# Layer 1's experts by blocks of one expert's tokens, in a four-layer transformer kernel on one core

## The chip, the cores and the metric

The kernel runs on 1 core of one Trainium2 chip. Its time is the device time of one execution in microseconds (us). Before the change it is 931.48 us, the median of 3 runs (926.2 to 931.48).

The engines are named as the profile names them: PE is TensorE (matrix products; PEld is its loading of weights), DVE is VectorE, ACT is ScalarE, POOL is GpSimd and SP is SyncE, which here only issues DMAs. Each engine works through a queue of its own in order.

## The reference, cut to what matters

The input x holds 16 sequences of 128 tokens with 128 features, in 32-bit floats. There are four layers. Each adds to x a gated attention of the normed x with a context, and then a gated feed-forward part of the normed x. `_layernorm` works on each token by itself.

```python
x = x + jnp.tanh(g_xattn[0]) * _L0_xattn_ref(_layernorm(x), ctx)           # linear attention
x = x + jnp.tanh(g_ffn[0])   * _L0_ffn_ref(_layernorm(x), ...)             # 8 experts, 2 of them per token
x = x + jnp.tanh(g_xattn[1]) * _L1_xattn_ref(_layernorm(x), ctx, ...)      # one head
x = x + jnp.tanh(g_ffn[1])   * _L1_ffn_ref(_layernorm(x), ...)             # 16 experts, 4 per token, 2 shared
x = x + jnp.tanh(g_xattn[2]) * _L2_xattn_ref(_layernorm(x), ctx, ctx, ...) # 16 heads, mask
x = x + jnp.tanh(g_ffn[2])   * _L2_ffn_ref(_layernorm(x), ...)             # 64 slots
x = x + jnp.tanh(g_xattn[3]) * _L3_xattn_ref(_layernorm(x), ctx, ctx, ...) # 16 heads, two scales
x = x + jnp.tanh(g_ffn[3])   * _L3_ffn_ref(_layernorm(x), ...)             # 32 experts, 8 per token, 1 shared
```

The part that the change is about is the feed-forward part of layer 1. An expert has a hidden width of 128.

```python
topk_idx, tw = _route(x, router_w, bias)   # sigmoid scores, the best 2 of 4 groups, then 4 of 16 experts
combine = (jax.nn.one_hot(topk_idx, 16) * tw[..., None]).sum(1)   # zero for 12 of 16 experts
h = jnp.einsum('td,edf->etf', x, gate_w)
u = jnp.einsum('td,edf->etf', x, up_w)
y = jnp.einsum('etf,efd->etd', jax.nn.silu(h) * u, down_w)
routed = jnp.einsum('etd,te->td', y, combine)
sh = jax.nn.silu(x @ sh_gate_w) * (x @ sh_up_w) @ sh_down_w
return routed + sh
```

Every token is multiplied with every expert here, and the products of 12 of the 16 experts get the weight zero.

## The kernel before, in words

The 16 sequences are four groups (0 to 3) of four sequences; a group is 512 tokens. `X[g]` holds a group's x in the core's memory all the time, as 128 partitions by 4 sequences by 128 features. A feed-forward part is computed for one group at a time, an attention likewise.

**Dense steps.** `experts` (L1028) walks over `ORDER`: layer 0 for group 0 only, layer 1 for groups 0 to 3, layer 3 for groups 0 to 3. For each of them it takes steps `n` over 128 hidden units each: 16 in layer 0, 18 in layer 1 (the 2 shared ones first), 17 in layer 3. `gated` (L440) issues a step's gate product (L445) and up product (L446), each with 512 columns; ACT applies the activation (L450, or L453 for silu), DVE forms `sg` (L451) and `h` (L457), and POOL or DVE multiplies `h` by the tokens' routing weights (`hw`, L461). `down` (L1033) adds the step's down product (L1036) to an accumulator, `LAG` = 2 steps later. At the end of a group `end` (L1042) transposes the sum (L1046) and adds it to X (L272). The PE instructions of this stream are held in order by `in_turn`.

**Routing.** `routing` (L839) norms a group (`normed`, L249: DVE, a power on POOL at L260, DVE at L264), transposes it (L244), computes the router's logits and weights (`weights_1`, L561, with `grouped_route`), and `spread` (L411) writes the weights to memory and loads each expert's row back, broadcast over all partitions (L428, 16 loads of 256 KB for layer 1).

**Blocks in layer 0.** Groups 1 to 3 of layer 0 (12 batches of 128 tokens) are computed otherwise. `choose_0` (L855) norms and transposes the three groups, computes all weights, counts on PE how many tokens chose each expert (L872 to L875), and gives each pair of token and expert a row in a table of 31 blocks of 128 rows, each block of one expert. POOL then scatters the tokens to these rows in the chip's memory by 24 indirect DMAs (L901), and each engine that needs it loads the blocks' weight positions into registers (L919). `blocks_0` (L930) loads four blocks of rows at a time (L959), transposes them (L966), copies the block's expert weights to a fixed place (L982), multiplies (L988), applies the activation (L995, L996), multiplies by the down weights (L943) and writes the rows to a second table (L951). `return_0` (L1008) fetches for each token its two rows by indirect DMAs on POOL (L1017, 24 of them) and adds them to X with their weights on DVE (L1024).

**What sets the order.** The attentions are issued by the main program (the loops at the end of the function), and `until` lets the stream of experts go on just far enough for the next attention. Inside `experts`, `steps` names the dense step after which a piece of another work is issued: pieces of `choose_0`, of `routing`, of `return_0` and of `slots_2` (layer 2's feed-forward part). A scheduler then orders each engine's queue: an instruction issued earlier in the program goes first among those that it reckons ready. `side` picks the PSUM banks: "m" for attention (four banks), "x" for experts (three banks), plus one bank for accumulators. Attention 2 of a group follows layer 1 of that group, attention 3 follows its slots, and layer 3 follows attention 3.

Of the kernel before, what the change touches and what calls it, by code (L numbers as in the profile page):

```python
# [36 lines left out]
NBLK = (2 * NT * P + 8 * (P - 1)) // P  # L37
# [22 lines left out]
def flamingo(ctx, tc, x_in, ctx_in, mask_in, w1, w2, w3, wslot, wsmall, slots, cols_in, rows_in, consts_in,  # L60
# [152 lines left out]
    xd, yd = [dram.tile([NBLK * P, D], F32, tag=n, name=n, bufs=1) for n in ("xd", "yd")]  # L213
    zeros, z0 = vp[:].rearrange("p t x -> p (t x)"), xd[:].rearrange("(p r) d -> p (r d)", p=P)
    for i in range(0, NBLK * D, GB * VB):
        n = min(GB * VB, NBLK * D - i)
        nc.scalar.dma_start(z0[:, i:i + n], zeros[:, :n])
# [12 lines left out]
    counted = const.tile([P, NBLK], I32, tag="counted", name="counted")  # L230
    nc.gpsimd.iota(counted[:], pattern=[[1, NBLK]], base=0, channel_multiplier=0)
    count = const.tile([P, NBLK], F32, tag="count", name="count")
# [5 lines left out]


# [9 lines left out]
    def normed(g, xn=None):  # L249
# [10 lines left out]
        nc.gpsimd.tensor_tensor(rs[:], ve[:], neghalf[:], ALU.pow)  # L260
# [13 lines left out]
    def add_row(g, r):  # L274
        nc.gpsimd.tensor_tensor(X[g][:], X[g][:], bc(r[:], 1, GB), ALU.add)
# [79 lines left out]
    def logits_of(xnT, w, n):  # L355
        p = split(mm_tile()[:, :GB * n])
        for t in range(GB):
            mm(p[:, t, :], xnT[:, t * P:(t + 1) * P], w)
        return p
# [23 lines left out]
    def grouped_route(p, bias, n, ngrp, top_grp, lt, fill, topk, tag, times):  # L383

        sc = small.tile([P, GB, n], F32, tag="sc", name="sc")
        nc.scalar.activation(sc[:], p, AF.Tanh, scale=0.5)
        nc.vector.tensor_scalar(sc[:], sc[:], 0.5, 0.5, ALU.mult, ALU.add)
        s = small.tile([P, GB, n], F32, tag="s", name="s", bufs=1)
        nc.vector.tensor_tensor(s[:], sc[:], bc(bias, 1, GB), ALU.add)

        s3 = s[:].rearrange("p t (g k) -> p (t g) k", g=ngrp)
        pairs = small.tile([P, GB * ngrp, 6], F32, tag="pairs", name="pairs", bufs=1)
# [3 lines left out]
        more, gs = room(GB, ngrp, top_grp if ngrp == 8 else 8, tag="gs", name="gs")  # L396
        nc.vector.tensor_reduce(gs, pairs[:].rearrange("p (t g) k -> p t g k", t=GB), AX.X, ALU.max)
        gm = first(more, ngrp, top_grp)[0] if ngrp == 8 else earlier_or_greater(gs, ngrp, lt, top_grp, "g" + tag)

        gf = small.tile([P, GB, ngrp], F32, tag="gf", name="gf")  # L400
        nc.vector.tensor_scalar(gf[:], gm[:], fill, fill, ALU.mult, ALU.subtract)
        more, m = room(GB, n, topk, tag="m", name="m", bufs=1)
# [4 lines left out]
        tw = small.tile([P, GB, n], F32, tag="tw", name="tw", bufs=1)  # L407
        nc.vector.tensor_tensor(tw[:], sc[:], sel[:], ALU.mult)
        return over_sum(tw, n, "comb", act, eps=1e-20, times=times)
# [29 lines left out]

    def gated(chain, w, xnT, cb, tanh, banks, vector):  # L440
# [409 lines left out]

    places = {}

    def choose_0():  # L855

# [171 lines left out]
    def experts():  # L1028
# [88 lines left out]
        while behind:  # L1117
            down()
# [216 lines left out]
```

## Time and profile before

| | |
|---|---|
| median of 3 runs | 931.48 us (926.2 to 931.48) |
| the profiled execution's own time | 930.84 us |
| its span in the profile | 929.1 us |
| mean granted PE clock | 0.965 |
| busy: PE, DVE, ACT, POOL | 90%, 62%, 28%, 30% |
| instructions | 16015 |
| moved by DMA | 62.12 MB, mean 67 GB/s |
| chain that ended last: PE, DVE, POOL, issue, ACT, DMA | 54%, 21%, 8%, 8%, 4%, 2% |

The ends of the groups can be read from the transposes at L1046. They start at 109.3 us (layer 0, group 0); 279.2, 370.8, 480.4 and 607.3 (layer 1, groups 0 to 3); 729.3, 816.9, 883.7 and 924.4 (layer 3, groups 0 to 3). The blocks of layer 0 run from 110 to 170 us.

How to read it: a group of instructions is given by line, engine, operation, the tiles written and read, the count, the busy time and the mean duration, and then the idle time of the engine before them with what ended it. "issue" means that nothing in the profile explains a wait. A 128x128 by 128x512 product in 32-bit floats appears as two PE records. In answers in order of time the first two numbers are the start and the length in us, and a bracket at the end is the idle time before.

### The profile page before, as it was taken

What the parts mean: (1) busy time and instruction counts of PE and PEld (TensorE: products, weight loads), DVE (VectorE), ACT (ScalarE), POOL (GpSimd) and SP (SyncE); (2) the same over time, 40 slices, a digit from 0 to 9 for tenths busy, and PEclk for the clock granted to TensorE, in tenths of its full rate; (3) what the DMA queues carried; (4) which work ended last, traced back from release to release, by engine and by line L of the source; (5) the groups of instructions that cost most, each with busy time, mean ns of one, the idle gap of its engine ahead of it and who ended that gap; (6) DMA issues with size and microseconds to landing.
All of it is one profiled execution on the core that took longest, in us unless ns stands there. A gap on an engine that the chain in (4) does not pass through costs nothing.

```text
span 929.1 us, 16015 instructions
## 1 busy us (share of the span) xinstructions
PE 834.3 (90%) x6183; PEld 468.5 (50%) x6183; DVE 580.6 (62%) x1628; ACT 259.3 (28%) x457; POOL 282.6 (30%) x283
## 2 busy tenths in 40 slices
PE   3889399877999999999899999999989998999997
PEld 3554289534544554455455555555554554554443
DVE  4756252566977475666675866677666668566622
ACT  1222166221321222232223222223222232322321
POOL 3326521353233124311421113421114223313443
PEclk9979699978999999999999999999999999999999
DMA  9711212552121012100202112310002111211231
GB/s 305 211 17 40 64 46 79 159 162 63 24 69 44 27 35 80 46 21 28 69 35 67 35 47 62 123 37 24 24 24 72 35 48 46 76 51 49 94 103 34
DMA packets 55677, 62.12 MB, mean 67 GB/s; under 512 B 14312, under 2 KB 33512, under 8 KB 55472
## 3 DMA queue, kind: packets, MB, share of 16 engines
q1 hardware_dynamic: 53776, 55.90, 19.9%
q0 software_dynamic: 1536, 3.15, 1.1%
q10 hardware_dynamic: 288, 2.03, 0.6%
q8 instruction: 49, 0.80, 0.4%
q14 instruction: 28, 0.23, 0.1%
HBM read 53.97 MB, written 7.09 MB: 66 GB/s over the span
## 4 chain that ended last, share of the span: by engine, by line
PE 54%; DVE 21%; POOL 8%; issue 8%; ACT 4%; DMA 2%; another core or an unknown queue 1%; SPq 1%; POOLq 0%; DVEq 0%; ACTq 0%
PE mm L108 8%; PE acc L1036 7%; PE pg L445 7%; PE pu L446 7%; POOL hw L461 3%; DVE sg L451 3%; PE mm L593 2%; PE po L487 2%; DVE h L457 2%; DVE mp L481 2%; POOL rs L260 2%; POOL y L1017 2%; DVE xn L264 2%; PE tr L244 2%; PE po L490 2%
## 5 line engine op out<-in xcount | busy, mean ns | idle before, releaser
L461 POOL TENSOR_TENSOR hw<-h,cb 128x512 f32<-128x512 f32 x126 | 161.0, 1278 | 459.4 <-DVE h L457 348.1
L446 PE MATMUL pu<-xnTx,wall 128*128 128x512 f32 x288 | 156.4, 626 | 14.9 <-DVE sg L451 13.1
L1036 PE MATMUL acc<-hw,wall 128*128 128x512 f32 x288 | 153.9, 618 | 10.6 <-DVE h L457 9.9
L445 PE MATMUL pg<-xnTx,wall 128*128 128x512 f32 x288 | 154.8, 620 | 7.8 <-issue 4.7
L450 ACT ACTIVATE sg<-pg 128x512 f32<-128x512 f32 x123 | 73.6, 598 | 244.7 <-PE pg L445 230.5
L457 DVE TENSOR_TENSOR h<-sg,pu 128x512 f32<-128x512 f32 x145 | 99.1, 683 | 60.9 <-PE pu L446 40.7
L451 DVE SCALAR_TENSOR_TENSOR sg<-sg,pg 128x512 f32<-128x512 f32 x123 | 83.6, 680 | 51.4 <-ACT sg L450 51.3
L1036 PEld LDWEIGHTS acc<-hw,wall 128*128 128x128 f32 x288 | 55.1, 198 | 71.3 <-issue 53.0
L446 PEld LDWEIGHTS pu<-xnTx,wall 128*128 128x128 f32 x288 | 52.4, 197 | 75.9 <-issue 39.1
L481 DVE TENSOR_REDUCE mp<-mm 128x4 f32<-128x512 f32 (+1 forms) x112 | 65.8, 645 | 21.1 <-PE mm L593 19.9
L445 PEld LDWEIGHTS pg<-xnTx,wall 128*128 128x128 f32 x288 | 50.1, 194 | 50.2 <-issue 35.1
L495 DVE RECIPROCAL rcw<-po 128x128 f32<-128x128 f32 (+1 forms) x28 | 25.2, 900 | 57.1 <-PE po L490 44.8
L264 DVE TENSOR_SCALAR xn<-x,mv,rs 128x128 f32<-128x128 f32 x116 | 40.3, 399 | 25.4 <-POOL rs L260 25.4
L615 ACT ACTIVATE pts<-mm 128x512 f32<-128x512 f32 x64 | 33.6, 602 | 73.3 <-PE mm L609 73.3
L487 PE MATMUL po<-pts,vp 128*32 128x128 f32 (+1 forms) x896 | 46.1, 274 | 7.6 <-ACT pts L615 6.7
L260 POOL TENSOR_TENSOR rs<-ve,neghalf 128x4 f32<-128x4 f32 x32 | 33.2, 1037 | 61.8 <-DVE ve L258 61.7
L490 PE MATMUL po<-pts,own 128*32 128x128 f32 (+1 forms) x896 | 44.3, 266 | 0.5 <-issue 0.5
L453 ACT ACTIVATE sg<-pg 128x512 f32<-128x512 f32 x33 | 19.7, 597 | 67.9 <-PE pg L445 58.4
L487 PEld LDWEIGHTS po<-pts,vp 128*32 128x32 f32 (+1 forms) x896 | 21.3, 108 | 29.9 <-ACT pts L615 14.0
L254 DVE BATCH_NORM_STATS2 st<-x 128x6 f32<-128x128 f32 x128 | 29.5, 280 | 10.2 <-DMA x<-in_x 9.9
L593 PE MATMUL mm<-kTm,qT 32*128 32x256 f32 x256 | 30.5, 413 | 0.0
L1017 POOL DMA_INDIRECT y<-yd,to x24 | 23.7, 987 | 21.7 <-DMA yd<-yb 8.8
(335 smaller groups left out, 1226.0 us busy)
## 6 DMA issues: line engine op xcount, KB each, us to landing
cb<-combD SPq DMA_DIRECT2D x72, 256.0 KB
cb<-combD SPq DMA_DIRECT2D x128, 128.0 KB
wall<-in_gu SPq DMA_DIRECT2D x24, 256.0 KB
wall<-in_dn SPq DMA_DIRECT2D x12, 256.0 KB
xb<-xd SPq DMA_DIRECT2D x7, 256.0 KB
yd<-yb SPq DMA_DIRECT2D x7, 256.0 KB
xd<-vp ACTq DMA_DIRECT2D x1, 1072.0 KB
x<-in_x SPq DMA_DIRECT2D x4, 256.0 KB
```

The source lines that it names most:

```text
L108: nc.tensor.matmul(out=o, lhsT=l, rhs=r, start=start, stop=stop)
L264: nc.vector.tensor_scalar(xn[:, t, :], x[:, t, :], mv[:, t, 0:1], rs[:, t:t + 1], ALU.subtract, ALU.mult)
L445: in_turn(chain, nc.tensor.matmul(out=pg[:], lhsT=w[:, 0], rhs=xnT[:], start=True, stop=True))
L446: in_turn(chain, nc.tensor.matmul(out=pu[:], lhsT=w[:, 1], rhs=xnT[:], start=True, stop=True))
L450: nc.scalar.activation(sg[:], pg[:], AF.Tanh, scale=0.5)
L451: nc.vector.scalar_tensor_tensor(sg[:], sg[:], 1.0, pg[:], ALU.add, ALU.mult)
L457: nc.vector.tensor_tensor(h[:], sg[:], pu[:], ALU.mult)
L461: (nc.vector if vector else nc.gpsimd).tensor_tensor(hw[:], h[:], cb[:], ALU.mult)
L481: nc.vector.tensor_reduce(mp[:, 0:n, 32 * i + 16:32 * i + 18], src, AX.X, ALU.max)
L487: in_turn(chain, nc.tensor.matmul(out=po[32 * jj:32 * jj + 32, 0, :], lhsT=vcols, rhs=pts, start=first, stop=last, skip_group_check=True))
L490: in_turn(chain, nc.tensor.matmul(out=po[32 * jj:32 * jj + 32, 1, :], lhsT=own[rows, r, :], rhs=pts, start=False, stop=last, skip_group_ch ...
L1036: in_turn(chain, nc.tensor.matmul(out=acc[0][:], lhsT=w[:, 2], rhs=h[:], start=n == 0, stop=last))
```

## The change

The new kernel treats groups 1 to 3 of layer 1 as layer 0 was treated. `choose_0`, `blocks_0` and `return_0` become `choose`, `blocks` and `fetch` for both layers.

- In layer 1 a token has four chosen experts, so the 12 batches need 48 scatters and 48 fetches, and the table has 63 blocks. A block of layer 1 has one gate, one up and one down product of 128 by 128 by 128; four blocks share a pass. Its weights are copied by POOL alone, two blocks to a tile. The activation is tanh on ACT and a product on DVE, as in layer 1's dense steps.
- Group 0 of layer 1 stays dense, with all `hw` products on DVE. Groups 1 to 3 run only the two shared steps densely (`stream(..., some=2)` with no routing weights): groups 1 and 2 right after group 0, group 3 after the blocks.
- The rows' table of layer 1 is filled with zeros by DMAs on SP in the program's opening part.
- `choose(1)` is issued after steps 10, 13, 15, 16, 17 and 17 of group 0; its first 12 scatters come with the last of these, the other 36 after the shared steps.
- `fetch` asks for four sets of four rows ahead, and adds one set at a time after named steps. By `behind_of`, an indirect DMA follows the latest power or row addition on POOL, an addition follows the latest `h` on DVE, and the first transposes of layer 1's blocks follow the last products of attention 2 of group 0.
- The later order is new: attention 2 of group 0, then the blocks with the slots of group 0 beside them, attention 3 of group 0, attention 2 of groups 1 and 2, attention 3 of group 1, attention 2 of group 3, attention 3 of groups 2 and 3. The slots of group g+1 go with layer 3 of group g. Layer 3's weights take the place of layer 1's after the blocks.
- The block positions are loaded into registers at the start of the blocks, at most 32 at a time.

```diff
-NBLK = (2 * NT * P + 8 * (P - 1)) // P
+EXPERTS, CHOSEN = {0: 8, 1: 16}, {0: 2, 1: 4}
+NBLK = {i: (CHOSEN[i] * NT * P + EXPERTS[i] * (P - 1)) // P for i in (0, 1)}
...
-        nc.gpsimd.tensor_tensor(rs[:], ve[:], neghalf[:], ALU.pow)
+        latest["row"] = nc.gpsimd.tensor_tensor(rs[:], ve[:], neghalf[:], ALU.pow).ins
...
+    def behind_of(what, ins):
+
+        if what in latest:
+            tc.add_manual_dep(ins.ins, latest[what].name,
+                              mybir.DependencyInfo(mybir.DependencyClass.NoSync, mybir.DependencyReason.DATA),
+                              reason="behind")
...
         for t in range(NT):
-            for k in range(2):
-                apart("xd", nc.gpsimd.indirect_dma_start(
-                    out=xd[:], out_offset=bass.IndirectOffsetOnAxis(ap=to[:, k, t:t + 1], axis=0), in_=xs[:, t, :],
-                    in_offset=None))
+            for i in range(k):
+                ins = nc.gpsimd.indirect_dma_start(
+                    out=xd[layer][:], out_offset=bass.IndirectOffsetOnAxis(ap=to[:, i, t:t + 1], axis=0),
+                    in_=xs[t // GB][:, t % GB, :], in_offset=None)
+                behind_of("row", ins)
+                apart(f"xd{layer}", ins)
+            if layer == 1 and t == 2:
+                yield
...
+        m, nc_ = (2, 2) if layer == 0 else (4, 1)
...
+                    ins = nc.tensor.transpose(pt[:, i * P:(i + 1) * P], xb[:, i, :], ident[:])
+                    if not chain and layer:
+                        behind_of("a2", ins)
+                    in_turn(chain, ins)
...
+                    half = wb[:, i % 2 * 2 * P:(i % 2 + 1) * 2 * P]
+                    src = wall[:, bass.ds(whose[b0 + i], 2 * CH)].rearrange("p (a f) -> p a f", a=2)
+                    copy(half.rearrange("p (a f) -> p a f", a=2), src[:, :, 0:P])
...
+    def fetch(layer):
+        to, by, _ = places[layer]
+        n = CHOSEN[layer]
+        held = []
+
+        def add():
+            g, y, k = held.pop(0)
+            for t in range(GB):
+                i = (g - BYE) * GB + t
+                ins = nc.vector.scalar_tensor_tensor(X[g][:, t, :], y[:, t, :], by[:, k, i:i + 1], X[g][:, t, :], ALU.mult,
+                                                     ALU.add)
+                behind_of("h", ins)
+            return g if k == n - 1 else None
...
+        todo = [(g, k) for g in range(BYE, NG) for k in range(n)]
+        for _ in range(4):
+            ask_next()
+        yield
+        while held:
+            yield add()
+
+            if len(held) in (2, 0) and todo:
+                ask_next()
+                ask_next()
...
+        at(steps, "x", fetch(0), RETURN_0, lambda g: g and (0, g))
+        at(steps, "m", ch, CHOOSE_1)
+        yield from stream(1, 0, *routed.pop((1, 0)), steps, moving=range(18))
+        for g in EARLY:
+            yield from stream(1, g, turned[g], None, {}, 2)
+        yield from flush()
+        side[0] = "m"
+        for _ in ch:
+            pass
+        sl = slots_2(0)
+        for n, _ in enumerate(blocks(1)):
+            side[0] = "s"
+            if n in SLOTS_0:
+                next(sl)
+                yield from shown(("slots", 0) if n == SLOTS_0[-1] else None)
+            side[0] = "m"
+        back, nxt = fetch(1), routing(3, 0)
+        side[0] = "x"
+        for step in (nxt, nxt, back):
+            next(step)
+        for g in range(BYE, NG):
+            if g not in EARLY:
+                yield from stream(1, g, turned[g], None, {}, 2)
+        if len(EARLY) < NG - BYE:
+            yield from flush()
+        for i in range(4):
+            side[0] = "x"
+            g = next(back)
+            yield from shown(g and (1, g))
+            side[0] = "x"
+            if i in (0, 1):
+                next(nxt)
+        loaded(3)
...
+    RETURN_0, CHOOSE_1 = (0, 3, 5, 6, 7, 9, 10), (10, 13, 15, 16, 17, 17)
+    EARLY = (1, 2)
+    SLOTS_0 = range(10)
+    RETURN_1 = (5, 6, 6, 7, 7, 8, 8, 9)
+    SLOTS = {1: (10, 11, 12, 12, 13, 13, 14, 15, 15, 16), 2: range(1, 11), 3: range(10)}
+    ROUTE_3 = (16, 16, 16, 16)
+    ATTEND = {0: ((2, 11), (3, 16))}
...
-    for g in range(NG + 1):
-        if g < NG:
+    for stage, g in ((2, 0), (3, 0), (2, 1), (2, 2), (3, 1), (2, 3), (3, 2), (3, 3)):
+        if stage == 2:
             until(1, g)
             attention_2(g)
-        if g > 0:
-            until("slots", g - 1)
-            attention_3(g - 1)
+        else:
+            until("slots", g)
+            attention_3(g)
```

## The prediction

> **What bounds the kernel now.** I read the page's busy table, then the costliest groups, then stages cut at the ends of the expert layers' token groups, then single engines in order of time where a stage showed a hole. TensorE (PE) is busy 90% of the span, and the dense expert matmuls lead the groups; an indirect DMA costs GpSimd (POOL) about 1 us.
>
> ```profile
> span 929.1 us, 16015 instructions
> PE 834.3 (90%) x6183; PEld 468.5 (50%) x6183; DVE 580.6 (62%) x1628; ACT 259.3 (28%) x457; POOL 282.6 (30%) x283
> ...
> L446 PE MATMUL pu<-xnTx,wall 128*128 128x512 f32 x288 | 156.4, 626 | 14.9 <-DVE sg L451 13.1
> L1017 POOL DMA_INDIRECT y<-yd,to x24 | 23.7, 987 | 21.7 <-DMA yd<-yb 8.8
> ```
>
> The stages follow (columns: stage, length, busy us of PE, PEld, DVE, ACT, POOL, granted clock, DMA share, GB/s). From 279.2 on PE is the bound in each. Only the stage in which layer 0's rows come back (170.4 to 215) has holes and a lower clock.
>
> ```profile
> 170.40:215.00 44.60, 31.88 (x76) 13.66 (x74) 23.03 (x64) 10.64 (x17) 26.02 (x27) 0.85 0.59 169
> 279.20:370.80 91.60, 86.60 (x645) 43.00 (x644) 59.51 (x137) 21.35 (x39) 25.53 (x23) 1.00 0.15 47
> 370.80:480.40 109.60, 103.56 (x749) 55.56 (x748) 74.32 (x184) 29.47 (x51) 28.64 (x27) 1.00 0.13 40
> 883.70:929.00 45.30, 40.14 (x99) 17.71 (x97) 11.75 (x17) 8.94 (x15) 18.97 (x15) 0.99 0.22 70
> ```
>
> The price of a dense step, from PE in order of time near the end, where nothing else runs: each of three matmuls is two records, and starts lie 0.86 us apart, so a step (gate, up, down) is 2.575 us.
>
> ```profile
> 894.43 1.02 PE L1036 MATMUL acc<-hw,wall 128*128 128x512 f32 x2
> 895.29 1.02 PE L445 MATMUL pg<-xnTx,wall 128*128 128x512 f32 x2
> 896.15 1.02 PE L446 MATMUL pu<-xnTx,wall 128*128 128x512 f32 x2
> 897.00 1.02 PE L1036 MATMUL acc<-hw,wall 128*128 128x512 f32 x2
> ```
>
> The price of blocks, from layer 0's: four blocks between two groups of transposes take 5.85 us (144.59 to 150.44). Eight records, four 128-column matmuls, take 0.89; four transposes 0.44.
>
> ```profile
> 144.59 0.60 PE L966 MATMUL tr<-ident,xb 128*128 128x128 f32 x4
> 145.03 1.06 PE L943 MATMUL acc<-wall,h 128*128 x8
> ...
> 150.44 0.60 PE L966 MATMUL tr<-ident,xb 128*128 128x128 f32 x4
> ```
>
> PE's waits while rows are fetched, and the pace of scatters on POOL (0.96 and a pause of 0.30: 1.263 us each):
>
> ```profile
> 184.33 2.08 PE L446 MATMUL pu<-xnTx,wall 128*128 128x512 f32 x2 [4.34 <-DVE sg L451]
> 192.69 2.07 PE L445 MATMUL pg<-xnTx,wall 128*128 128x512 f32 x2 [4.74 <-issue]
> 217.66 2.08 PE L446 MATMUL pu<-xnTx,wall 128*128 128x512 f32 x2 [5.17 <-DVE sg L451]
> ```
> ```profile
> 102.66 0.96 POOL L901 DMA_INDIRECT xd<-xs,to  x1 [0.30 <-issue]
> 103.93 0.95 POOL L901 DMA_INDIRECT xd<-xs,to  x1 [0.30 <-issue]
> ```
>
> **The change part by part.** The sum is made in the profiled execution (span 929.1, its own time 930.84, so 1.7 beside the span); the median of the runs is 931.48, 0.6 above it.
>
> *Work taken from PE.* Layer 1 ran 18 dense steps for each of four groups. Groups 1 to 3 keep 2 shared steps each; 48 steps go: 48 x 2.575 = 123.6 us. In come at most 63 blocks. Four of them are 12 matmuls and four transposes, 3 x 0.89 + 0.44 = 3.12 us, so 63/4 x 3.12 = 49.2 us. Three routings leave (transposes 0.43, logits 0.80, spread 0.44: 1.7 each); the choice for twelve batches brings 12 transposes, logits and a count that took 2.9 us in layer 0 (66.70 to 69.60; 3.5 taken for twice the columns), together 7.2. PE is 72 us lighter. The other engines also lose: 48 times 1.36 us on VectorE (DVE), 0.60 on ScalarE (ACT), 1.28 mostly on POOL.
>
> *Until the fourth group leaves attention 1.* The last block of layer 0 ends at 170.4 and I move nothing before it. Its block names are now loaded at the blocks' start (one load took 2.6 to 3.0 us on each queue); PE stood still 9.9 us there in the profile, which covers it. If that cover goes, it costs 3. The zeros for layer 1's rows (4 MB, four DMAs on SP) go out beside a DMA share of 0.25 or less; cost 0, at most 10. Fetches now stand behind the latest GpSimd row operation and additions behind the latest h, so the three PE waits shown (4.34 + 4.74 + 5.17 = 14.2 us) should mostly go. Attention 1 of group 3 ended at 271; I take 257, with bounds of 250 (the clock of 0.85 recovers too) and 271 (no gain: all hw products of group 0 move to DVE, six more of 0.69, where DVE was busy 51.7 of 64.2).
>
> *The new scatter.* After 257 everything goes through one chain: norm 4.6 (281.7 to 286.3), transposes and copy 1.7, logits and tanh 1.2, choice 10 (6.9 for four batches, 161.98 to 168.85; twelve have three times the columns, so 6.9 to 13), counts 3.5, places 4.8 (69.78 to 74.62): 25.8. Then 48 scatters at 1.263 = 60.6, then landing, load and first transpose 5.3 (104.88 to 110.19). First block at 257 + 91.7 = 349, bounds 339 and 363. Attention 2 of group 0 lies beside it (281.7 to 338.9 in the profile, with dense steps in its gaps), the four early shared steps too, but there is no further dense work. Roughly 30 us of PE idle is the price of this place. In POOL's queue attention 2's power and row operations stand before the 36 later scatters, by the added dependency; the first 12 can hold them 15 us, which is inside the bounds.
>
> *From the first block on.* From 279.2 to the end was 649.9 us. Attention 2 of group 0 with 18 steps is over by then: minus its stage, 91.6. Of the other 36 steps two shared ones stay: minus 34 x 2.575 = 87.6. Blocks: plus 49.2. Two routings: minus 3.4. Idle that went with the removed work (stages from 370.8: busy 522.9 of 558.3, 6.4%): minus 2.7. Rest: 514.
>
> *Fetching back.* A last copy out lands after 5.1 us (170.9 to 176.0), 16 gathers of 1.25 give 20, the last landing and additions 3: 28 us from the last block to attention 2 of group 1. Cover: two shared steps (5.2), routing 1.7, the rest of attention 3 of group 0, and layer 3's first steps if its weights (3.1 MB, behind the last block now, at some 176 GB/s) have come. Bounds 5 and 28; I take 16. The other 32 gathers lie beside attention 2 of group 1. The 48 additions (0.34 each, 16 us) go to DVE, which loses more than that; they cost something only if one waits for its rows at the head of DVE's queue, in the bound.
>
> *Order of later stages.* Attention 3 of group 1 now runs with layer 3's group 0 spent and group 1 not routed; attention 3 of group 0 took 38 us with about six dense steps in it (470 to 509). Plus 8, between 0 and 12. SP's queue loses 51 DMAs of the three spreads (48 of 256 KB) and gains 32 block loads and stores; nothing new stands in front of a weight load but these. The copies of block weights (63 on POOL, half of a 0.61 us copy) lie under PE; the final group is unchanged.
>
> *Clock.* After a hole the same matmul pair took 2.08 instead of 1.02 us for about two pairs: plus 2, between 0 and 6.
>
> Sum: 349 + 514 + 16 + 8 + 2 = 889, plus 1.7 beside the span: 891 us. All low ends give 339 + 514 + 5 + 1.7 = 860, all high ends 363 + 514 + 28 + 12 + 6 + 1.7 = 925.
>
> **A rule that speaks against the change.** The trace shows scatters at 0.96 us (24 of them, 1.23 at most) though DVE was busy 8.4 of 16 us beside them (76 to 92). The Trainium skill's page "SBUF — State Buffer", section "SBUF: two separate sides", says that descriptors of a DMA issued from GpSimd cannot be written while VectorE holds the shared port in a two-port mode. The page gives 3100 against 620 ns; 64 DMAs on the path with 2.5 us more each would make the sum about 1050, an estimate from that page that no row here supports.
>
> **Rivals.**
> 1. *The scatter's hole is filled*: slots and attention 3 of group 0 need only attention 2 and could run before the blocks, so some 30 us return, partly lost again in the fetch (10), while the remaining fetch wait hides: 891 - 30 = 861. For: both are emitted early in the block stage. Against: the blocks' first transposes are emitted before them, and PE takes its queue in order.
> 2. *Slower*: indirect DMAs beside busy attention take longer. The place is POOL, 48 scatters and the first 16 gathers on the path. From 0.63 us more each (1.9 instead of 1.263) the gain is gone; doubled, 64 x 1.26 = 81, 972 us. For: a gather took 1.51 once, and tiny VectorE operations (128x4, 0.17) took 1.14 beside POOL work. Against: the medians, 0.958 and 0.952.
> 3. *PE's queue waits twice in full*: attention 2 of group 1 stands before layer 3's steps while its rows come, and the choice gains nothing: 349 to 363 (+14), fetch at 28 (+12), attention 3 at 12 (+4): 921. For: PE waited for h or sg three times in the first return. Against: shared steps are put between.
> 4. *Blocks save less than they should*: PE matmul time isn't the block's limit, four blocks take layer 0's 5.85 us, for three PSUM banks serve gate, up and transposes. Plus 15.75 x 2.73 = 43: 934. For: only the three banks. Against: per four blocks DVE has 1.4, ACT 1.8, POOL 1.3 us, and layer 0's 61 us stage was 98% busy.
>
> **How the numbers follow.** Forecast 0.48 (its own range 870 to 910), rival 1 0.17, rival 2 0.10, rival 3 0.17, rival 4 0.08. About 1% is what a measurement of this kernel can tell from no change: below 922 is faster, above 941 slower. Faster: forecast, rival 1 and most of rival 3 (0.13): 0.78. Same: the rest of rival 3 and most of rival 4: 0.10. Slower: rival 2 and the tail of rival 4: 0.12. The range 852 to 930 takes in both ends of the sum and rivals 1 and 3; it leaves out rival 2, rival 4 and a little below, 0.18 to 0.2.
>
> **What would show it.** PE matmul records fall by 48 x 6 and rise by 63 x 7 or so; four blocks take about 3.1 us; 48 scatters run at 1.26 us in one row of POOL with PE idle some 30 us before the first block near 349; a hole of 10 to 20 us on PE before attention 2 of group 1; no PE wait over 4 us in layer 0's return. It would be wrong if scatters stretch, if the hole before the blocks is filled, or if PE stands before layer 3's first group for longer than 28 us.

## The result, and the profile after

The changed kernel takes 1056.24 us (median of 4 runs, 1051.29 to 1059.9) against 931.48 (median of 4, 926.2 to 931.88): ratio 1.1351, 95% interval 1.1289 to 1.1413. The prediction was 891, with a range of 852 to 930. It was wrong by 165 us and on the wrong side.

The page of the changed kernel first (columns as before). PE is less busy, as the change wanted, but by 22 us (834.3 before) and not by the 72 of the prediction, and in a longer span, at a mean granted clock of 0.874 (0.965 before). The 48 new scatters (and 24 old ones) keep their 0.97 us. New is the last entry of the L510 line: PE idle ahead of attention 2's weighted products, ended by "issue", by nothing that the profile shows.

```profile
span 1054.4 us, 16557 instructions
...
PE 812.1 (77%) x6350; PEld 500.7 (47%) x6350; DVE 570.0 (54%) x1630; ACT 256.6 (24%) x451; POOL 316.5 (30%) x371
...
L938 POOL DMA_INDIRECT xd<-xs,to x72 | 70.0, 973 | 30.0 <-issue 21.3
...
L510 PE MATMUL po<-pts,own 128*32 128x128 f32 (+1 forms) x896 | 52.8, 288 | 24.2 <-issue 24.2
```

Then the stages of the changed kernel (stage, length, busy us of PE, PEld, DVE, ACT, POOL, clock, DMA share, GB/s), cut at the end of layer 1's group 0, at the first block, at the end of the shared steps of group 3, at the first exponentials of attention 2 of group 1, at the end of layer 3's group 0 and at its last.

```profile
272.50:397.30 124.80, 61.04 (x566) 35.19 (x565) 42.62 (x142) 11.15 (x20) 53.90 (x65) 0.70 0.09 32
397.30:501.60 104.30, 93.69 (x1024) 79.77 (x1022) 61.06 (x144) 41.44 (x73) 26.39 (x59) 0.97 0.30 89
501.60:557.00 55.40, 19.31 (x82) 9.78 (x85) 24.53 (x89) 3.07 (x6) 31.48 (x34) 0.66 0.30 98
557.00:784.20 227.20, 192.27 (x2074) 110.24 (x2067) 141.68 (x350) 50.03 (x93) 37.20 (x35) 0.89 0.08 26
784.20:1049.70 265.50, 220.68 (x1574) 118.76 (x1572) 137.31 (x362) 64.25 (x113) 70.24 (x57) 0.89 0.14 45
```

Three stretches stand out. From 272 to 397 PE does 61 us of work in 125: the transposes of the first block start at 397.3 and not at 349. From 502 to 557, while rows are fetched, it does 19 in 55. The last stretch, from layer 3's group 0 to its last group, takes 265.5 us; before the change it took 195.1 (729.3 to 924.4), and the change does not touch its dense steps.

What stands still in the first stretch is seen on PE in order of time (start, length, the idle time ahead in the bracket). The products of attention 2 first come eight at a time, then one by one, and the time between two starts grows from 0.7 to 3.5 us. Nothing that the profile shows explains these waits: the bracket names no engine. GpSimd's row of scatters lies beside it, from 291.3 to 352.

```profile
310.71 0.65 PE L507 MATMUL po<-pts,vp 128*32 128x128 f32 x8
311.14 0.64 PE L510 MATMUL po<-pts,own 128*32 128x128 f32 x4
312.67 0.37 PE L510 MATMUL po<-pts,own 128*32 128x128 f32 x1 [0.89 <-issue]
...
320.45 0.37 PE L507 MATMUL po<-pts,vp 128*32 128x128 f32 x1 [1.03 <-issue]
...
331.68 0.37 PE L507 MATMUL po<-pts,vp 128*32 128x128 f32 x1 [2.43 <-issue]
...
355.48 0.37 PE L510 MATMUL po<-pts,own 128*32 128x128 f32 x1 [3.12 <-issue]
```

**The theories.** *Hold-up*: beside a long row of indirect DMAs the other engines get their instructions late, so that attention 2 of group 0 hides nothing of the row. *Order* (the rival): the loss lies in the later order, where attention, slots and routing of a group now stand one after the other, and the dense steps that were taken away had been their cover. Both turned out true: the first is worth 53 us, and only on some chips, the second 66 to 86 us, by the way it is counted.

### The profile page after: what moved, and what is told of

Same layout as the page of the kernel before. It is cut to its first block, busy times and chain, and to the rows that moved or that the text cites. A ratio compares the mean times of both kernels' runs of the same rounds, so it can differ in the third digit from the quotient of the medians.

```text
span 1054.4 us, 16557 instructions
## 1 busy us (share of the span) xinstructions
PE 812.1 (77%) x6350; PEld 500.7 (47%) x6350; DVE 570.0 (54%) x1630; ACT 256.6 (24%) x451; POOL 316.5 (30%) x371
## 4 chain that ended last, share of the span: by engine, by line
PE 24%; DVE 11%; issue 9%; POOL 6%; ACT 1%; DMA 1%; another core or an unknown queue 1%; POOLq 0%; DVEq 0%; ACTq 0%
PE mm L109 4%; PE pg L464 3%; POOL y L1117 3%; PE pu L465 3%; PE acc L1144 3%; DVE mp L501 2%; PE po L507 2%; POOL hw L481 1%; PE po L510 1%; PE mm L612 1%; DVE h L476 1%; POOL rs L268 1%; PE tr L109 1%; PE mm L774 1%; DVE rep L362 1%
## 5 line engine op out<-in xcount | busy, mean ns | idle before, releaser
L481 POOL TENSOR_TENSOR hw<-h,cb 128x512 f32<-128x512 f32 x61 | 77.8, 1276 | 277.5 <-DVE h L476 258.4
L465 PE MATMUL pu<-xnTx,wall 128*128 128x512 f32 x192 | 105.0, 630 | 14.4 <-DVE sg L470 7.7
L1144 PE MATMUL acc<-hw,wall 128*128 128x512 f32 x192 | 103.5, 624 | 6.5 <-DVE hw L481 4.8
L464 PE MATMUL pg<-xnTx,wall 128*128 128x512 f32 x192 | 104.9, 629 | 3.3 <-DVE h L476 3.3
L476 DVE TENSOR_TENSOR h<-sg,pu 128x512 f32<-128x512 f32 x97 | 66.3, 684 | 62.2 <-PE pu L465 47.8
L1117 POOL DMA_INDIRECT y<-yd,to x72 | 70.7, 982 | 80.5 <-DVE x L1097 45.6
L469 ACT ACTIVATE sg<-pg 128x512 f32<-128x512 f32 x75 | 44.8, 597 | 203.9 <-PE pg L464 182.0
L938 POOL DMA_INDIRECT xd<-xs,to x72 | 70.0, 973 | 30.0 <-issue 21.3
L470 DVE SCALAR_TENSOR_TENSOR sg<-sg,pg 128x512 f32<-128x512 f32 x75 | 51.0, 682 | 41.0 <-ACT sg L469 40.9
L510 PE MATMUL po<-pts,own 128*32 128x128 f32 (+1 forms) x896 | 52.8, 288 | 24.2 <-issue 24.2
L510 PEld LDWEIGHTS po<-pts,own 128*32 128x32 f32 (+1 forms) x896 | 30.9, 119 | 26.4 <-issue 25.9
```

Of the source, the lines that this page charges most:

```text
L464: in_turn(chain, nc.tensor.matmul(out=pg[:], lhsT=w[:, 0], rhs=xnT[:], start=True, stop=True))
L465: in_turn(chain, nc.tensor.matmul(out=pu[:], lhsT=w[:, 1], rhs=xnT[:], start=True, stop=True))
L470: nc.vector.scalar_tensor_tensor(sg[:], sg[:], 1.0, pg[:], ALU.add, ALU.mult)
L476: ins = nc.vector.tensor_tensor(h[:], sg[:], pu[:], ALU.mult)
L481: (nc.vector if vector else nc.gpsimd).tensor_tensor(hw[:], h[:], cb[:], ALU.mult)
L510: in_turn(chain, nc.tensor.matmul(out=po[32 * jj:32 * jj + 32, 1, :], lhsT=own[rows, r, :], rhs=pts, start=False, stop=last, skip_group_ch ...
```

## The experiments

Each group of kernels below ran on one chip, with a run of the kernel before that took 927 to 933 us on every one of them. The chips are lettered in the order of their use. Except for the kernel of layer 0's new return (chip B), each kernel ran once in its group; one of them, the changed kernel without scatters, ran on two chips and took 990.43 and 992.09 us. "The record" means the runs of the first section, whose chip was not noted.

### Chip A: the change's parts, and the row of scatters by itself

*The kernel before without the 48 dense steps.*

```diff
+                if not (layer == 1 and g >= BYE and n >= 2):
                     banks = [bank("pg", wide), bank("pu", wide)]
...
+                                                stop=n == 1 if cut else last))
```

> The kernel before, in which groups 1 to 3 of layer 1 compute only their two shared steps (48 dense steps are left out, everything else keeps its place). This prices what the change took from TensorE without anything that it added. By the prediction's own terms: 48 x 2.575 = 123.6 us come off the path, so 808 us. By the rival theory that dense steps were the cover of attention chains, and TensorE merely waits where they stood: only about half comes off, 860 to 880 us.

845.25 us: 86.3 came off, not 123.6. The rival was half right about the cover (its 860 to 880 was too high). In the stretch from layer 1's group 0 to layer 3's group 0, PE's idle time rose from 25.9 us (450.1 minus 424.2) to 46.3 (364.7 minus 318.4). Its busy time there fell by 105.8 us and not by 123.6: the matmuls that stayed took longer (the 512 products of L609 302 ns each for 283), at a granted clock of 0.94 where it was 1.00.

*The changed kernel without layer 1's scatters, and without scatters, blocks and fetches.*

```diff
-            for i in range(k):
+            for i in range(k if layer == 0 else 0):
...
-        for n, _ in enumerate(blocks(1)):
+        for n, _ in enumerate([None] * 16):
```

> The changed kernel without layer 1's 48 scatters (its blocks read the zeros of the table, so layer 1's routed part of groups 1 to 3 is missing from the output); all else is unchanged. Theory 1 (the row of scatters holds up attention 2 of group 0 beside it): attention 2 of group 0 runs its 57 us from 297 on, and the blocks start some 58 us earlier: 1056 - 58 = 998 us. Theory 2 (attention 2 waits for something else): the blocks start where they did, since they stand behind attention 2 of group 0: 1045 to 1056 us.

990.43 us, 66 less than on record; this seemed to fit the hold-up, but the 1056 comes from another chip (see chip F).

> The changed kernel without layer 1's scatters, blocks, fetches and additions (the routed part of groups 1 to 3 is missing from the output); the choice, the shared steps, the slots and the later order stay. It prices the later order beside the kernel before without its 48 dense steps, which does the same work. If the order costs little, the two lie within 20 us (the return of layer 0 is better here). If the order is the larger part of the loss (attention and routing one after the other with no dense steps in their gaps), this one is 50 us or more above it, about 880 to 900 us.

931.42 us, 86 us above the kernel before without its 48 steps, which does nearly the same work (three routings of layer 1 where this one has the choice): the order is expensive, more than expected. Its last stretch takes 263.4 us (661.4 to 924.8); in the kernel before without its steps it takes 193.1. So 70 of the 86 us lie there, with no block, scatter or fetch of layer 1 in the kernel at all: 36 us more busy time of PE (219.1 for 183.0; the slots of one more group now stand in this stretch) and 34 us more idle time. Blocks and fetches together cost 990.43 - 931.42 = 59.

*A row of indirect DMAs by itself.*

> A kernel of its own that computes nothing of the reference: ten phases one after the other, each with the same chain of 24 turns (eight small matmuls on TensorE, one tanh on ScalarE, one addition on VectorE). Beside it GpSimd's queue holds, phase by phase: nothing; 48 scatters; 48 gathers; 48 copies; 24 scatters with a copy after each; 48 scatters of 64-byte rows; 48 direct writes from GpSimd's queue; 48 direct writes from SP's queue; 12 scatters; nothing. Theory 1 (a long unbroken row of indirect DMAs holds up the instructions of the other engines, whatever they wait for): the phases with 48 scatters and 48 gathers take clearly longer than the first, as a turn that takes 2 to 3 us runs at a fraction of its pace from about the 15th DMA on, and recovers after the 48th (60 us of DMAs, so a phase of 55 us grows to about 100); the phases with copies, with SP's writes and with 12 scatters keep the first phase's length within 5 us. Theory 2 (the engines waited in the changed kernel for something in GpSimd's own queue, or for data): all phases keep the first one's length within 5 us, or reach the series' 60 us and no more.

All phases took 122.8 to 124.8 us (the last, which also writes the output, left out), with the 48 scatters 122.8 and with the copies 124.8. No hold-up: theory 2 seemed right, but the later chips show that this was one on which no row held anything up.

### Chip B: halves, and a denser chain

> The first of these kernels of its own showed no effect of a row of 48 indirect DMAs on a chain that issues 18 instructions in 5 us. This one computes nothing of the reference either: seven phases with the same chain of 12 turns, each of 64 tiny matmuls, four tanh and four additions, so that every engine issues many more instructions in a microsecond; beside it GpSimd's queue holds nothing, 48 scatters, 48 gathers, 48 copies, 24 scatters with a copy after each; then SP's queue 48 direct writes; then nothing. Theory 1a (while indirect DMAs run in a row, new instructions reach the engines at a limited pace, some 0.7 us each, once those at hand are used up): the phases with 48 scatters and 48 gathers are longer than the first by 30 us or more, those with copies and SP's writes are not. Theory 1b (the hold-up has to do with where the real kernel's tables and instructions lie, or with what its queue holds, and not with the DMAs as such): all seven phases have one length within 5 us.

The phases took 339.4 us alone, **382.0 beside 48 scatters, 383.4 beside 48 gathers**, 339.5 beside 48 copies, 339.8 beside 24 scatters with a copy of 512 elements after each (1.77 us each), 339.6 beside SP's 48 writes. This is theory 1a, and the same picture as in the kernel. PE in order of time, in the phase with scatters (row from 344.0 to 404.4):

```profile
354.83 9.11 PE L114 MATMUL ps<-a,ident 128*128 128x8 f32 x42
364.60 0.17 PE L114 MATMUL ps<-a,ident 128*128 128x8 f32 x1 [0.66 <-issue]
...
371.66 0.38 PE L114 MATMUL ps<-a,ident 128*128 128x8 f32 x1 [1.24 <-issue]
...
391.29 0.17 PE L114 MATMUL ps<-a,ident 128*128 128x8 f32 x1 [2.63 <-issue]
...
411.59 2.08 PE L114 MATMUL ps<-a,ident 128*128 128x8 f32 x9 [0.32 <-issue]
```

For 20 us matmuls follow each other at 0.21 us; then one comes each 0.7, 1.4, 2.1 and 2.8 us, steps of 0.70; 7 us after the row's last DMA all is as before.

*Half the scatters, and no fetches.*

```diff
-            for i in range(k):
+            for i in range(2):
```

> The changed kernel with 24 of layer 1's 48 scatters (two of a token's four rows; half of the routed part of groups 1 to 3 is missing from the output). Without any scatter it was 990 us, with all 1056. If attention 2 of group 0 is held up for as long as the row lasts beyond its first dozen DMAs, half the row gives about 1056 - 30 = 1026. If what costs is a threshold (a row of 24 is still harmless), it falls to the 990 of no scatter at all, give or take 6.

1027.15 us, 29 less than on record, with the first block at 364.6: a row of 24 is not harmless, as the first reading had it. (The changed kernel itself did not run on this chip.)

> The changed kernel without layer 1's 48 fetches and their additions (the routed part of groups 1 to 3 is missing from the output); scatters and blocks stay. By the prediction's term the fetch costs 16 us (5 to 28): 1056 - 16 = 1040. If its row of indirect DMAs holds up the routing of layer 3's group 0 beside it, as the profile of the changed kernel suggests (TensorE waits from 502 to 535), and later rows do the like: about 1056 - 40 = 1016. It also shows whether the hold-up of attention 2 of group 0 by the 48 scatters, which stay, comes again.

1006.44 us, 50 less than on record, where the prediction had 16 for the fetch. PE in the changed kernel on record stands for 32 us where layer 3's first routing (on DVE) runs beside the first 24 fetches on POOL. The same wait is 20.5 us on chip F, so that some 12 us of it go with the hold-up:

```profile
502.08 0.98 PE L109 MATMUL mm<-wsmall,xnTx 128*128 128x32 f32 x8
535.44 1.03 PE L428 MATMUL tr<-ident,comb 128*32 128x128 f32 x4 [32.38 <-DVE comb L384]
```

*One part alone: layer 0's new return in the kernel before.*

```diff
-                for i in range(BYE, NG):
-                    back = return_0(i)
...
+                back = fetch(0)
+                for n in (0, 3, 5, 6, 7, 9, 10):
+                    steps.setdefault(n, []).append(("x", back, lambda g: g and (0, g)))
```

> One part alone: the kernel before (layer 1 dense for all groups, its order unchanged) with the new return of layer 0 (four sets of rows asked ahead, one place added at a time, GpSimd's fetches behind its latest row operation, additions behind the latest h). In the changed kernel group 0 of layer 1 ended at 272.5 instead of 279.2. If that gain is kept to the end: 931.5 - 6 = 925. If later waits take it up: 931 within 2.

926.29 us (10 runs) beside 930.87 (13 runs): ratio 0.9951, interval 0.9925 to 0.9976. The gain of this part is real and is kept to the end. Of the kernels that compute the whole output it is the fastest here, below both the one before and the changed one.

### Chip C: pace, and the later order

> The dense chain by itself again (it computes nothing of the reference), beside rows of scatters of different length and pace: 16 in a row; 24 in a row; 48 with a copy of 32 elements after each; 48 with a copy of 128 elements; 48 with a copy of 512 elements; 48 with eight copies of 512 elements after every eighth; nothing. In the run before, 48 in a row cost the chain about 43 us, and 24 with a copy of 512 elements after each cost nothing. If what counts is the number in an unbroken row (the hold-up began with the 15th or 16th), 16 cost 0 to 5 us, 24 cost 10 to 15, and the 48 that are broken up by a pause, in the fourth to sixth phase, cost under 5. If what counts is the mean pace, a small copy doesn't help (the third phase costs 40, the fourth 20 to 40) and the fifth and sixth cost nothing.

339.4 to 342.3 us in all phases but the last, which also writes the output; so neither reading could be told from it: this chip shows no hold-up (the next kernel confirms it).

*The later order altered.*

```diff
-    SLOTS = {1: (10, 11, 12, 12, 13, 13, 14, 15, 15, 16), 2: range(1, 11), 3: range(10)}
-    ROUTE_3 = (16, 16, 16, 16)
-    ATTEND = {0: ((2, 11), (3, 16))}
+    SLOTS = {0: ((1, (10, 10, 11, 11, 12, 12, 13, 13, 14, 14)), (2, (14, 14, 15, 15, 15, 16, 16, 16, 16, 16))),
+             1: ((3, range(1, 11)),), 2: ()}
+    ROUTE_3 = {0: (16, 16, 16, 16), 1: (6, 8, 10, 12), 2: (6, 8, 10, 12)}
+    ATTEND = {0: ((2, 11), (3, 15))}
```

> The changed kernel with one part of its later order altered: the slots of group 2 go with layer 3 of group 0 (behind those of group 1) and those of group 3 with layer 3 of group 1, and the routing of groups 2 and 3 moves from step 16 of the group before to steps 6 to 12. From the end of layer 3's group 0 to the end of the kernel took 195 us before the change and 265 to 270 after it, in every variant run so far, with scatters, blocks and fetches or without. If that stretch is what the order costs there (slots, attention 3, routing and dense steps of one group one after the other), 40 to 60 us of the 70 come back: about 1005. If attention and slots only move to an earlier stretch that is as empty: 1045 to 1056.

964.93 us, more than expected. The trace showed why: here attention 2 of group 0 was not held up by the same 48 scatters, and the first block started at 356. The scatters of layer 0, which every kernel has, tell the same of the chips. ACT, late in that row, in the profile of the kernel before that the prediction was made from:

```profile
97.44 0.60 ACT L453 ACTIVATE sg<-pg 128x512 f32<-128x512 f32 x1 [7.72 <-issue]
108.64 0.58 ACT L1039 COPY yT<-acc 128x512 f32<-128x512 f32 x1 [10.61 <-remote]
```

and the second of them on chip A (the kernel before without the 48 steps, which come later):

```profile
97.70 0.59 ACT L1042 COPY yT<-acc 128x512 f32<-128x512 f32 x1 [2.90 <-PE acc L1038]
```

In the kernel before, DVE waited beside ACT (9.80 us, "issue"), and PE for DVE: the 9.9 us that the prediction counted as cover belong to the hold-up. It costs nothing at that place, for the blocks wait for the same row (on chip A PE waited 12.9 us for it instead); so the kernel before takes the same time on all chips. ACT's copy waited for 7 to 14 us in all seven kernels of the record, chip B and chip D that have no pauses in the row, and for 2.90 us in all seven of chips A, C, E and F.

### Chip D: the changed kernel, its order and its pace side by side

> The changed kernel as it is, on the same chip as the three that follow. So far the hold-up of the engines beside a long row of indirect DMAs showed in every kernel of some calls (each call has one chip) and in none of others, though the kernels of both kinds hold the same rows. Theory 1c (the hold-up goes with the chip or with where it places the program, and the change has two separate costs: the hold-up there, and the later order everywhere): where it is absent the changed kernel takes 1056 less the 50 us by which attention 2 of group 0 and the blocks start later: 1000 to 1010, and its first block starts near 357 us. Theory 1d (it goes with the kernel): 1056 as before.

> The altered later order again, beside the changed kernel on one chip. By theory 1c the order itself is worth 1005 - 965 = 40 us, whatever the chip: 965 where the changed kernel takes 1005, and about 1015 where it takes 1056. By theory 1d it is 965 beside 1056.

1056.24 and 1015.64 us. The chip holds the engines up (PE again comes one matmul at a time), and the altered order is worth 40.6 us on it, as theory 1c had it. The expectations of chips E and F put the first block near 410 and 412 where the engines are held up; its transposes start at 397.4 here and at 397.3 on record, 40 us later than on chip F.

*A pause behind each indirect DMA.*

```diff
+        m = nc.gpsimd.tensor_copy(pace[:], count[:, 0:32])
+        tc.add_manual_dep(m.ins, ins.ins.name,
```

> The changed kernel with a copy of 32 elements on GpSimd behind each scatter and each fetch, which took 0.22 us in a kernel by itself and stretched the pitch from 1.263 to 1.37 us. If an unbroken row is what holds the engines up, and they are held up on this chip, it comes to about 1005 where the changed kernel takes 1056. If the pause does nothing, or nothing is held up here, it is 0 to 6 us above the changed kernel on the same chip (48 scatters 5 us later).

> Both edits: the altered later order and the copy behind each indirect DMA. If both are right and separate: 965 to 970 on any chip. If the pause does nothing, the same as the altered order on this chip, within 6 us.

1055.35 and 1012.99 us: a pause of that size gains nothing in time, and an unbroken row is not the condition. Yet it changes the hold-up. With the pause ACT's copy at layer 0's row of 24 waited for 2.93 and 2.95 us, where the two kernels without it on this chip waited for 10.57 and 7.12; and in layer 1's row PE comes one matmul at a time only from 341 on, some 45 us after the row's start and not 20 (before that stands one wait of 4.4 us), though ACT's second set of exponentials came at 338.1, 8.5 us after the matmuls that it needed. The row lasts 5.6 us longer for the pause, and the first block starts at 395.9.

### Chip E: more pace

> The dense chain by itself once more (nothing of the reference is computed): beside it 48 scatters in a row; 16; 24; 48 with one copy of 32 elements after each (pitch 1.37 us); 48 with three such copies; 48 with a copy of 512 elements (1.77 us); 48 with eight copies of 512 elements after every eighth; 48 direct writes from GpSimd's queue; nothing. The first phase says whether this chip is of the kind that holds the engines up: it is then some 40 us longer than the last; if it is not, no phase is. On a chip of that kind: if a queue fills because DMAs come faster than something drains, 16 cost nothing, 24 little, the pitch of 1.37 still 30 us or more (as in the real kernel, where it gained 1 us), the pitch of 1.77 nothing; if the unbroken row counts, every phase with copies costs nothing.

339.4 to 342.0 us in all phases but the last, also beside 48 in a row: a chip without the hold-up, so the question of pace stays open.

> The altered later order with three copies of 32 elements behind each indirect DMA instead of one (pitch about 1.9 us). If the pace is what holds the engines up and this chip does so: attention 2 of group 0 runs through, the blocks begin when the row ends, near 291 + 48 x 1.9 + 5 = 387 instead of some 410 us, and the fetch's neighbours run on: 985 to 1000, against 1013 to 1016 for the same order with one copy or none. On a chip without the hold-up: 965 plus the longer row, 985 to 1000.

1052.44 us, 87 above the same order without pauses on chip C, and well above what was expected: layer 0's rows are longer too, the first scatter of layer 1 moves from 290.9 to 327.5, and 96 us of row lie on the path. Where nothing is held up, a slower pace only costs.

### Chip F: the changed kernel where nothing is held up

> The changed kernel as it is on one more chip. Where the chip holds the engines up beside long rows of indirect DMAs: 1056, first block near 412 us. Where it doesn't: the altered order took 965 there and gained 41 us on a chip that does, so 1005, and the first block near 357.

> The changed kernel without layer 1's 48 scatters (the routed part of groups 1 to 3 is missing from the output), beside the changed kernel on one chip. On a chip without the hold-up 990 again, so that the scatters cost some 15 us there; on one with it the fetches' rows still hold things up: 1000 to 1010, and the scatters cost about 50.

1002.95 and 992.09 us. So the changed kernel took 53 us more on the record's chip and on chip D than here, and the 48 scatters cost 11 us where nothing is held up. The stretch of 40 us that shows it, first in the changed kernel on record, then on chip F (PE 6.6 against 17.5 us):

```profile
320.00:360.00 40.00, 6.58 (x30) 2.53 (x29) 0.00 (x0) 0.60 (x1) 28.60 (x38) 0.50 0.18 62
```
```profile
320.00:360.00 40.00, 17.45 (x239) 12.22 (x240) 8.20 (x15) 4.82 (x9) 29.43 (x39) 0.71 0.19 66
```

On chip F attention 2's exponentials run on, one sequence after the other:

```profile
300.70 1.57 ACT L634 ACTIVATE pts<-mm 128x512 f32<-128x512 f32 x3 [9.93 <-PE mm L628]
...
313.36 1.57 ACT L634 ACTIVATE pts<-mm 128x512 f32<-128x512 f32 x3 [10.20 <-PE mm L628]
...
325.09 1.57 ACT L634 ACTIVATE pts<-mm 128x512 f32<-128x512 f32 x3 [9.16 <-PE mm L628]
```

## Why the prediction was wrong, point by point

Chip F lets the error be split in the prediction's own execution (its 889 us are a span; chip F's is 1001.2, the one on record 1054.4).

- **Until the first block: right, without the hold-up.** 349 forecast (339 to 363), 357.5 on chip F; the row began at 292.4 where the sum has 282.8. It ran at 1.26 us for a scatter and PE waited 16.9 us in one piece for its rows, while attention 2 of group 0 lay beside it as said. Layer 1's group 0 ended at 272.5 on record (279.2 before), without the three waits of 4 to 5 us in layer 0's return. The first block of the record came at 397.3.
- **From the first block to the end of layer 3's group 0: 38 us missed.** The prediction's terms give 358.5 - 87.6 + 49.2 - 3.4 - 2.7 + 16 + 8 + 2 = 340; chip F took 378.3 (357.5 to 735.8). The step that failed is "48 x 2.575 = 123.6": dense steps were priced by a place where nothing else runs. Their removal in the kernel before gave 86.3. Of the 37 that did not come, some 20 are idle time (cover for chains that then wait in the open) and some 18 longer matmuls. The fetch failed in the same direction: PE stood some 29 us of 61 on chip F, just above the 5 to 28, where I took 16:

```profile
450.70:512.00 61.30, 31.83 (x177) 18.10 (x175) 32.83 (x114) 8.37 (x16) 34.10 (x36) 0.72 0.41 120
```

  How much of the 38 is cover and how much is fetch was not separated. The 38 is also too kind to this stretch, for slots that stood in it before the change now stand in the last one.
- **The later order: 66 us missed.** "Plus 8, between 0 and 12" looked at attention 3 of group 1 alone and took the last stretch as unchanged. It went from 195.1 to 260.7 us. Before, on chip F, and with the altered order on chip C:

```profile
729.30:924.40 195.10, 184.62 (x1360) 93.64 (x1358) 113.95 (x293) 53.82 (x96) 64.93 (x52) 0.99 0.19 61
```
```profile
735.80:996.50 260.70, 216.14 (x1573) 115.99 (x1571) 137.33 (x362) 64.28 (x113) 70.25 (x57) 0.91 0.15 46
```
```profile
742.10:958.50 216.40, 198.05 (x1509) 104.76 (x1507) 121.35 (x319) 57.57 (x104) 67.19 (x54) 0.97 0.19 55
```

  Some 32 us are more PE time (slots of groups 2 and 3 now stand in this stretch, before only those of group 3, and the clock is 0.91 for 0.99), some 34 are more idle time. So a part of the 66 is work moved here and no loss of the order; it was not priced by itself. Its largest waits, on chip F, are for routing and slots, which nothing covers; in the kernel before no wait of that kind is above 2.1 us in total:

```profile
PE tr L428 <- DVE comb L384: 14.3, 2, 7.2
PE tr L252 <- DVE xn L272: 9.0, 4, 3.7
PE mm L109 <- DVE combs L384: 7.6, 2, 3.8
PE mm L109 <- POOL ns L700: 6.4, 2, 3.2
```

  With the slots a group ahead and the routing in mid-stream, 44 of the 66 us came back there, and 38 of them in the whole kernel (964.93 against 1002.95).
- **The hold-up: 53 us, a term that the prediction put at nothing.** It let attention 2 of group 0 lie beside the row and priced the row alone. On record the first block starts 39.8 us later than on chip F, the exponentials of attention 2 of group 1, behind the first fetches, 45.6 us later (557.9 against 512.2), and the end comes 53.2 us later; the last 7.6 us of this were not traced. 8.5 + 38.3 + 65.6 + 53.2 = 165.6 is the whole error of 165.4.
- **"PE is 72 us lighter" and "Clock: plus 2, between 0 and 6": both wrong by some 40 us.** This is another cut through the same 112 us that were missed on chip F, not a further term. The matmul records came as forecast (6350; 6183 - 48 x 6 + 63 x 7 is 6336), but PE's busy time fell only from 834.3 to 802.8 us, at a mean granted clock of 0.895 for 0.965. So some 40 us are longer PE time and some 72 more idle time than the sum had. After a wait the same pair of records took 1.92 us and a little later 1.02 (chip F):

```profile
494.28 1.25 PE L252 MATMUL tr<-ident,xn 128*128 128x128 f32 x4 [7.13 <-DVE xn L272]
495.32 1.92 PE L464 MATMUL pg<-xnTx,ws 128*128 128x512 f32 x2
...
500.39 1.02 PE L109 MATMUL mm<-xnTm,w2h 128*128 128x512 f32 x2
```

- **The blocks: right.** Four blocks took 1.00, 0.89 and 0.98 us for the three products and 0.44 for the transposes, 3.3 us where the sum has 3.12; the rest of the time belongs to slots of group 0 (chip F):

```profile
372.55 1.16 PE L1062 MATMUL pg<-xbT,wb 128*128 128x128 f32 x8
373.55 1.06 PE L1062 MATMUL pu<-xbT,wb 128*128 128x128 f32 x8
374.44 0.60 PE L1026 MATMUL tr<-ident,xb 128*128 128x128 f32 x4
374.88 1.06 PE L1003 MATMUL acc<-wall,h 128*128 x8
375.86 1.10 PE L109 MATMUL tr<-slots,hTs 64*128 64x64 f32 x8
```

- **The rivals.** Rival 2 had the sign, the place and roughly the time, but the mechanism reversed: not the indirect DMAs take longer beside a busy attention (48 scatters 954 to 1138 ns), the attention does beside them. So the rule of the Trainium skill's page "SBUF — State Buffer", section "SBUF: two separate sides", found no row here either: on record the row keeps its 1.26 us while VectorE is idle (0.00 of 40 us), and on chip F its scatters took 954 to 1137 ns beside a VectorE that was busy for 8.2 of 40 us; no run shows whether these operations were of the kind that the page means. The hint was in the trace: 7.72 and 10.61 us ahead of ACT late in layer 0's row, with no engine to blame; I read the row's own durations and not its neighbours'. Rivals 1 and 4 did not come about: nothing filled the hole, and the three PSUM banks did not limit the blocks. Rival 3 came about in its fetch (29 us against its 28) and nearly in its first block (357.5 against 363), but the 30 us that it puts on the forecast are about a quarter of the 112 that were missed without the hold-up.

## What to carry to other kernels

A dense step that fills the gaps of a latency chain is worth less than its length: before such work is removed, take it out of the kernel and nothing else, and see what is left to gain. Here it was 86 us; blocks and fetches took 59 of it and the scatters 11, which left 16 for a later order that cost 86. When a change moves work, price every later stage again with the new cover, the untouched ones too. When two operations are to run side by side, read in the trace how the neighbours of such a row fared, not only the row.

## What the runs showed of the hardware

- On chips B and D and in the runs of the record (whose chip may be one of these) a row of 48 indirect DMAs, scatters or gathers, held the other engines' instructions up: TensorE's from about the 15th DMA on, one instruction each 0.70 us or a multiple of it, until about 7 us after the row's end. ScalarE was held earlier: on record its first exponential came at 309.2, though the matmuls that it needed had ended at 299.7, beside the 7th DMA. The DMAs themselves kept their 0.96 us. On four others (A, C, E, F) rows of indirect DMAs held up nothing; two programs ran on a chip of each kind, the changed kernel on D and F and the altered order on C and D. What holds the instructions up is not shown: the profile has only waits without a releaser. Whether the chip itself decides or where a program and its tables lie on it is not settled, and neither is whether an execution that the profiler doesn't record is held up too, for every run here has the profiler's span and clock.
- On chip B 24 scatters at 1.77 us each, 48 copies on GpSimd and 48 writes from SP held up nothing. At about 1.4 us each, on chip D, a row of 24 did not hold ACT up, and one of 48 still held ACT up for 8.5 us and PE from some 45 us on. Whether 1.77 would do for 48 on such a chip was not tried.
